# Counting equal entries instead of gathering 47 columns of values, and no power operation behind gathers once the table is whole

## The chip, the cores and the metric

The kernel runs on one core of a Trainium2 chip. Such a core has TensorE (PE; its weight loads are PEld), VectorE (DVE), ScalarE (ACT), GpSimd (POOL) and SyncE (SP), which only issues DMAs here. The metric is the device time of one execution in microseconds; lower is better. A profile is one such execution, recorded by the hardware.

## The reference, cut to what matters

Two layers of a graph network over N = 2708 nodes with D = 128 features. `adj` is a dense 2708 x 2708 array, but only about five entries of a row (on average) are not zero: each row is a 0/1 mask with ones on the diagonal, divided by its number of ones. So all entries of a row that are not zero are the same number, the one on the diagonal.

```
# layer 0: hyperbolic aggregation, dense product with adj
XW = mobius_matvec(W, X); gamma = 2 / max(1 - |XW|^2, 1e-5)
two_mean = (adj @ (gamma * XW)) / clamp(adj @ (gamma - 1))
x = layernorm(x + expmap0(relu(logmap0(scale(two_mean)))))
# layer 1: messages over the pairs with adj[i, j] != 0
s = x @ msg_w[:, :D].T ; d = x @ msg_w[:, D:].T
messages = gelu(s[:, None, :] + d[None, :, :] + msg_b)      # i, j, d
aggregated = einsum('ijd,ij->id', messages, adj)
h = gelu(concat([x, aggregated]) @ upd_w.T + upd_b) + x
x = layernorm(x + layernorm(h) * ln_w + ln_b)
```

## The kernel before, in words

**Tiling.** The nodes lie in NB = 22 blocks of 128. `adj_t` is adj transposed by blocks with the diagonal set to zero; the diagonal itself comes as `dg`, one column for each block.

**Layer 0** (`layer0`, L362) takes one block b a turn: SP loads `aT` (128 x 2816, 1408 KB, two buffers of the pool `stream`), ACT takes its Sign (`sgn`, L367), and PE multiplies 22 pieces of `aT` with `y` (L372). Three calls of `layer0_end` (after blocks 10, 20 and 22) turn the sums into the new x, and write the product that every message needs as a row for each node into `table_dram` (L596, seven writes).

**Finding the pairs.** From `sgn`, `keys` (L388) and `extract` (L425) list the pairs (i, j) with adj[i, j] not zero, packed into 99 columns ("tiles") of 128 pairs. `LISTS` gives each list its number n of tiles and how many of them are `late`: the first n - late tiles hold only columns j below SPLIT*P = 1280, the late ones only columns from 1280 on. By the list `LATE` 48 of the 99 tiles are late. For each tile `extract` leaves `J` (the column), `rid` (the row), `same` (the value of row i's diagonal) and `F` (the flat address of adj[i, j], L513).

**Two gathers for each tile**, both indirect DMAs issued by POOL through `gather` (L197): `V` fetches adj[i, j], 128 single words, and `dd` fetches 128 rows of 512 bytes of `table_dram`. V is not used in the sum: at the end L895 compares V with `same`, and a mismatch sets a flag under which a dense loop does layer 1 over again (L905). The message uses `same` as the weight. Behind two of every three gathers stands an operation on POOL that only spends time: `gap`, a power of a 128 x 1 column (L205).

**When gathers go out.** In `extract`, V of a block below AT_ONCE = 12 goes out at once; that of later blocks is held in `values` and goes out one a turn (L815), two a message (L776), or when no rows are left to fetch (L734). Rows of early tiles need only the first 1280 rows of the table and start in block 14 (`fetch(6)`, L814). `whole` becomes true once the whole table is written in the source; only then are late rows fetched (L827). RING = 14 buffers of four tiles hold fetched rows.

**Messages** (`messages`, L741) take four tiles a turn: PE selects the s rows (L751), DVE builds the weighted selection `rv` (L753) and adds the gathered rows (L756), ACT applies Gelu (L757), PE sums into the nodes (L766). There are 25 such groups: 11 of the early tiles of blocks 0 to 13, then 14 of the rest. `node`, `update`, `first` and `finish` (L616 to L682) then do a block's update and its two normalisations, and write `out`.

**Order.** Each engine runs its instructions in the order that the framework's scheduler fixes at build time; it starts from the source's order, but lets instructions that are ready earlier go ahead. `tc.issue_after(ins)` holds instructions of an engine behind `ins`.

Of the kernel before, what the change touches and what calls it, by code (L numbers as in the profile page):

```python
# [28 lines left out]
CHUNKS = [(0, 10), (10, 20), (20, 22)]  # L29
PARTS = (0, 1, 2, 2)  # L30
GROUPS = [(0, 8), (8, 6), (14, 4), (18, 2), (20, 2)]
AT_ONCE = 12
EARLY = 14
FETCH = 14

# [46 lines left out]
def hyperbolic_then_message_kernel(  # L82
# [17 lines left out]
    LISTS, NT, NC = lists()  # L100
    CMAX = max(v[3] + v[4] for v in LISTS)
    NL = len(LISTS)
    TMAX = max(TILES)

    const = ctx.enter_context(tc.tile_pool(name="const", bufs=1))
# [62 lines left out]
    R = big.tile([P, NT, P], BF16, name="R")  # L168
    J = const.tile([P, NT], U32, name="J")
    V = const.tile([P, NT], F32, name="V")  # L170
    rv_of = const.tile([P, NT, 2], F32, name="rv_of")
    rid, same = rv_of[:, :, 0], rv_of[:, :, 1]
    top = const.tile([P, NC], F32, name="top")
# [6 lines left out]
    nc.gpsimd.memset(deg, 0.0)  # L180
    oe = const.tile([P, NL, 2], F32, name="oe")
    signs = const.tile([P, NB], F32, name="signs")
    poss = const.tile([P, NL], F32, name="poss")
    cap = const.tile([P, NL], F32, name="cap")
    least = const.tile([P, NL], F32, name="least")
# [11 lines left out]
    def gather(o, src, at, kind):  # L197
        last = nc.gpsimd.indirect_dma_start(  # L198
            out=o, out_offset=None, in_=src, in_offset=bass.IndirectOffsetOnAxis(ap=at, axis=0)
        )  # L200
        gathers[0] += 1
        latest[:] = [last.ins]
        if gathers[0] % 3:
            with tc.issue_after(last.ins), tc.high_priority():
                nc.gpsimd.tensor_tensor(gap[kind], half, half, op=OP.pow)  # L205

# [154 lines left out]

    def layer0(b):  # L362

        aT = stream.tile([P, NB, P], F32, name="aT")
        nc.sync.dma_start(aT, adj_t[b])
        sgn = stream.tile([P, NB, P], BF16, name="sgn")
        nc.scalar.activation(sgn, aT, AF.Sign, accum_out=signs[:, b : b + 1])  # L367
        op = bank("mp", 3)
        for j in range(NB):
            if j in BREAKS:  # L370
                yield
            p = nc.tensor.matmul(  # L372
                op[:, : D + 2], lhsT=aT[:, j, :], rhs=y[:, j, :], start=(j == 0), stop=(j == NB - 1)
            )
        products.append(p)

        nc.vector.scalar_tensor_tensor(
            nom[:, b, :], y[:, b, :], dg[:, b : b + 1], op[:, : D + 2], op0=OP.mult, op1=OP.add
        )
        v, t = nom[:, b, :D], small.tile([P, D], F32, name="junk")  # L380
        nc.scalar.activation(t, v, AF.Square, accum_out=ss[:, b : b + 1])
        t = small.tile([P, D], F32, name="junk_p", bufs=1)
        nc.vector.scalar_tensor_tensor(
            t, v, 0.0, v, op0=OP.max, op1=OP.mult, accum_out=sp[:, b : b + 1]
        )
        yield sgn
# [38 lines left out]
    def extract(l):  # L425
# [68 lines left out]
        for k0 in range(0, n, step):  # L494
# [18 lines left out]
            nc.vector.scalar_tensor_tensor(  # L513
                F[:, k0:k1], J[:, t], float(b * P * N - 1), rid[:, t], op0=OP.add, op1=OP.add
            )
        values.extend((t, F[:, t - t0 : t - t0 + 1]) for t in range(t0, t0 + n))
        if b < AT_ONCE:
            value(n)
        known[0] = b
# [152 lines left out]
    def node(h, k, b, b0, n, more, pool=fin):  # L672
# [7 lines left out]
        if k == n - 1:  # L680
            yield
            yield from finish(h, b0, n, pool, last=(b == NB - 1))  # L682

    queue = []

    def step(n=NB):
# [54 lines left out]
    def messages():  # L741

        q, ts = done[0], work[done[0]]
        done[0] += 1
        w = len(ts)
        dd = rooms[q][:, :w, :]
        X = bank("kx" if q >= ahead and q % 2 else "X").rearrange("p (t d) -> p t d", d=D)[:, :w, :]
        rv = edge.tile([P, 4, P], F32, name="rv", bufs=2)
        for k, (b, t, *_) in enumerate(ts):
            for i in range(3):  # L750
                nc.tensor.matmul(X[:, k, :], lhsT=R[:, t, :], rhs=s3[:, b, i, :], start=(i == 0), stop=(i == 2))  # L751

            nc.vector.tensor_scalar(  # L753
                rv[:, k, :], iotaN, rid[:, t : t + 1], same[:, t : t + 1], op0=OP.is_equal, op1=OP.mult
            )
        nc.vector.tensor_tensor(dd, X, dd, op=OP.add)  # L756
        nc.scalar.activation(dd, dd, AF.Gelu)  # L757
        for k, (b, t, first, final, before) in enumerate(ts):
            mine = before or b >= EARLY
            if first:  # L760
                while len(sums) > 2:
                    step()
                sums[b] = bank("mp", 3)
                if mine:
                    own(b, sums[b])
            nc.tensor.matmul(  # L766
                sums[b][:, :P], lhsT=dd[:, k, :], rhs=rv[:, k, :], start=(first and not mine), stop=final
            )
            if final and before:
                nc.scalar.copy(gd[:, b, :D], sums.pop(b)[:, :P])  # L770
            elif final:
                g0, gn = group[b]
                queue.append(node(gd[:, g0 : g0 + gn, :D], b - g0, b, g0, gn, [gd[:, b, :D]] if b < EARLY else []))
        fetch()
        if not whole:
            value(2)  # L776
        step()
        step(1)

# [9 lines left out]
    with tc.issue_after(setup.ins):  # L789
        for b in range(NB):  # L790
            block = layer0(b)
            next(block)
            go_on(b, 0)
            for x in placed:
                next(x, None)
            placed = []
            next(block)
            go_on(b, 1)
            for x in found:
                next(x)  # L800
            placed, found = found, []
            sgn = next(block)
            for l in of_block[b]:
                keys(l, sgn)
                found.append(extract(l))
            if b == 0 or b == NB - 1:
                for x in found:
                    next(x)
                    next(x, None)
                for x in placed:  # L810
                    next(x, None)
                found, placed = [], []
            if b >= FETCH:
                fetch(6)  # L814
                value(1)  # L815
            for b0, b1 in CHUNKS:
                if b == b1 - 1 and b1 < NB:
                    ends.append((b1, layer0_end(b0, b1)))
                    next(ends[-1][1])
    for _, e in ends:  # L820
        for _ in e:
            pass
# [64 lines left out]
    while done[0] < len(work):  # L887
        messages()
    value(NT)
    while queue:  # L890
        step()


    differ = small.tile([P, 4 * P], F32, name="work", bufs=3)[:, :NT]
    nc.vector.tensor_tensor(differ, V, same, op=OP.not_equal)  # L895
    nc.vector.scalar_tensor_tensor(differ, rid, 0.0, differ, op0=OP.is_gt, op1=OP.mult)
    other = small.tile([P, 3], BF16, name="db")
    nc.vector.tensor_reduce(other[:, 0:1], differ, axis=AX.X, op=OP.max)
    bp = bank("sel", 1)
    nc.tensor.matmul(bp[:, 0:1], lhsT=ones_b, rhs=other[:, 0:1], start=True, stop=True)  # L900
    flag = sc.tile([P, 1], I32, name="flag")
# [3 lines left out]
    with tc.If(dense > 0):  # L905
        with tc.tile_pool(name="dn", bufs=1) as dn:
            room = R.rearrange("p t i -> p (t i)").bitcast(F32)
            dT, sT = (flat(stream.tile([P, NB, P], F32, name="aT")) for _ in range(2))
            agT, row = (room[:, k * NP : (k + 1) * NP] for k in range(2))
            ge = flat(mx)  # L910
            nc.vector.memset(agT, 0.0)
# [95 lines left out]
```

## Time and profile before

| what | us |
|---|---|
| median of 3 runs | 397.85 (396.5 to 399.37) |
| the profiled execution | 396.73 |
| its span, first to last instruction | 395.0 |
| POOL busy | 290.8 |
| PE busy | 286.8 |
| DVE busy | 280.8 |
| ACT busy | 215.7 |
| last matmul of layer 0 (L372) starts | 217.8 |
| last write of the table is issued | 257.96 |
| first Gelu of a message (L757), last one | 241.6, 361.6 |

How to read it: the span is cut by engines that wait for each other, so busy shares are averages over stages with different limits; the chain of waits that ended last, and the engines' order of time in each stage, say more. In the lines shown below, a group has the source line, the engine, the operation, the tile that is written and those that are read, the count, the busy time and the mean, and the idle time of the engine just before with what ended it. The TensorE clock is a share of full speed. Line numbers are those of the kernel before.

### The profile page before, as it was taken

What the parts mean: (1) busy time and instruction counts of PE and PEld (TensorE: products, weight loads), DVE (VectorE), ACT (ScalarE), POOL (GpSimd) and SP (SyncE); (2) the same over time, 40 slices, a digit from 0 to 9 for tenths busy, and PEclk for the clock granted to TensorE, in tenths of its full rate; (3) what the DMA queues carried; (4) which work ended last, traced back from release to release, by engine and by line L of the source; (5) the groups of instructions that cost most, each with busy time, mean ns of one, the idle gap of its engine ahead of it and who ended that gap; (6) DMA issues with size and microseconds to landing.
All of it is one profiled execution on the core that took longest, in us unless ns stands there. A gap on an engine that the chain in (4) does not pass through costs nothing.

```text
span 395.0 us, 8366 instructions
## 1 busy us (share of the span) xinstructions
PE 286.8 (73%) x2616; PEld 255.7 (65%) x2616; DVE 280.8 (71%) x1579; ACT 215.7 (55%) x614; POOL 290.8 (74%) x424
## 2 busy tenths in 40 slices
PE   3418989989998999899998287399738569738100
PEld 3307988888987879788888266298636459626000
DVE  0798889977668979667579989877534547559632
ACT  2982676878757859777767469254212222242201
POOL 5500188888888883788888888888888888888830
PEclk9856999999999999989999778689887997975555
DMA  8800554444454545455662122101111111130101
GB/s 308 338 1 2 182 205 170 177 153 147 170 216 180 191 156 183 161 187 168 220 251 65 41 55 75 33 15 36 41 42 40 40 42 41 42 95 15 40 0 52
DMA packets 16031, 45.17 MB, mean 114 GB/s; under 512 B 5418, under 2 KB 10942, under 8 KB 13166
## 3 DMA queue, kind: packets, MB, share of 16 engines
q1 hardware_dynamic: 9502, 37.43, 25.9%
q0 software_dynamic: 6336, 6.55, 7.0%
q10 hardware_dynamic: 144, 0.60, 0.5%
q8 instruction: 22, 0.36, 0.3%
q14 instruction: 27, 0.22, 0.2%
HBM read 41.74 MB, written 2.83 MB: 113 GB/s over the span
## 4 chain that ended last, share of the span: by engine, by line
POOL 31%; PE 23%; DVE 20%; DMA 10%; issue 8%; ACT 5%; another core or an unknown queue 1%; DVEq 0%; POOLq 0%; ACTq 0%
POOL dd L198 14%; POOL gap L205 9%; PE mp L372 9%; POOL V L198 8%; DMA dd<-table_dram,J 6%; PE mp L766 3%; PE sel L501 3%; PE kx L399 2%; DMA table_dram<-dt 2%; DVE top L407 2%; DVE dd L756 2%; DMA xT<-in_x_t_dram 1%; ACT dd L757 1%; DMA V<-in_adj_dram,F 1%; PE sel L621 1%
## 5 line engine op out<-in xcount | busy, mean ns | idle before, releaser
L198 POOL DMA_INDIRECT V<-in_adj_dram,F x99 | 99.4, 1004 | 59.2 <-DVE F L513 38.2
L372 PE MATMUL mp<-y,aT 128*128 128x130 f32 x968 | 131.1, 286 | 0.3 <-issue 0.3
L372 PEld LDWEIGHTS mp<-y,aT 128*128 128x128 f32 x968 | 118.7, 195 | 0.9 <-issue 0.6
L198 POOL DMA_INDIRECT dd<-table_dram,J x99 | 98.1, 990 | 22.4 <-issue 19.7
L205 POOL TENSOR_TENSOR gap<-gap 128x1 f32<-128x1 f32 x132 | 82.3, 623 | 3.2
L367 ACT ACTIVATE sgn<-aT 128x2816 bf16<-128x2816 f32 x22 | 56.0, 2548 | 1.5 <-issue 0.9
L766 PE MATMUL mp<-rv,dd 128*128 128x128 f32 x198 | 35.0, 329 | 27.2 <-ACT dd L757 25.9
L766 PEld LDWEIGHTS mp<-rv,dd 128*128 128x128 f32 x198 | 29.8, 229 | 30.5 <-ACT dd L757 28.6
L399 PE MATMUL kx<-kd,sgn 128*128 128x128 bf16 x484 | 33.2, 224 | 8.1 <-ACT sgn L367 8.1
L399 PEld LDWEIGHTS <-sgn 128*128 128x128 bf16 x484 | 28.3, 100 | 14.4 <-ACT sgn L367 8.5
L757 ACT ACTIVATE dd<-dd 128x512 f32<-128x512 f32 (+1 forms) x25 | 15.6, 623 | 33.7 <-DVE dd L756 31.7
L753 DVE TENSOR_SCALAR rv<-iotaN,rv_of 128x128 f32<-128x128 f32 x99 | 30.7, 353 | 3.5 <-PE mp L766 3.5
L407 DVE MAX8 top<-kx 128x8 f32<-128x128 f32 (+3 forms) x133 | 25.4, 228 | 10.4 <-remote 5.5
L468 ACT ACTIVATE away<-iota,mid 128x256 f16<-128x256 f32 (+3 forms) x54 | 28.5, 571 | 3.8 <-DVE mid L461 2.9
L756 DVE TENSOR_TENSOR dd<-X,dd 128x512 f32<-128x512 f32 (+1 forms) x18 | 12.2, 679 | 20.6 <-DMA dd<-table_dram,J 19.7
L501 PE MATMUL sel<-z,R 128*128 128x42 bf16 (+5 forms) x297 | 19.3, 192 | 10.1 <-DVE R L473 5.3
L501 PEld LDWEIGHTS <-R 128*128 128x128 bf16 x297 | 15.0, 96 | 14.6 <-DVE R L473 7.3
L751 PEld LDWEIGHTS <-R 128*128 128x128 bf16 x297 | 21.6, 106 | 1.9 <-issue 0.3
L411 ACT ACTIVATE junk_s<-kx 128x384 bf16<-128x384 f32 (+2 forms) x25 | 12.1, 486 | 13.2 <-DVE top L407 10.4
L751 PE MATMUL X<-s,R 128*128 128x128 bf16 x213 | 18.6, 232 | 0.0
L756 DVE TENSOR_TENSOR dd<-kx,dd 128x512 f32<-128x512 f32 x7 | 4.8, 691 | 17.5 <-DMA dd<-table_dram,J 17.5
L506 DVE TENSOR_TENSOR work<-sel,place 128x120 f32<-128x120 f32 (+11 forms) x29 | 11.1, 384 | 8.5 <-PE sel L501 8.4
(226 smaller groups left out, 596.2 us busy)
## 6 DMA issues: line engine op xcount, KB each, us to landing
aT<-in_adj_t_dram SPq DMA_DIRECT2D x22, 1408.0 KB
V<-in_adj_dram,F POOLq DMA_INDIRECT x99
dd<-table_dram,J POOLq DMA_INDIRECT x99
xT<-in_x_t_dram SPq DMA_DIRECT2D x2, 704.0 KB
x_sb<-in_x_nm_dram SPq DMA_DIRECT2D x2, 704.0 KB
table_dram<-dt SPq DMA_DIRECT2D x4, 256.0 KB
out_dram<-nom SPq DMA_DIRECT2D x4, 256.0 KB
pk<-in_pack_dram ACTq DMA_DIRECT2D x1, 587.5 KB
```

Of the source, the lines that this page charges most:

```text
L198: last = nc.gpsimd.indirect_dma_start(out=o, out_offset=None, in_=src, in_offset=bass.IndirectOffsetOnAxis(ap=at, axis=0))
L205: nc.gpsimd.tensor_tensor(gap[kind], half, half, op=OP.pow)
L367: nc.scalar.activation(sgn, aT, AF.Sign, accum_out=signs[:, b : b + 1])
L372: p = nc.tensor.matmul(op[:, : D + 2], lhsT=aT[:, j, :], rhs=y[:, j, :], start=(j == 0), stop=(j == NB - 1))
L399: nc.tensor.matmul(kp[:, i * P : (i + 1) * P], lhsT=sgn[:, j, :], rhs=kd[:, q, :], start=False, stop=(i == len(groups) - 1 and j == j1 - 1),)
L407: nc.vector.max(top[:, c : c + 8], seg[:, s, :])
L468: nc.scalar.activation(r0, iota[:, k0 * P : k1 * P], AF.Abs, scale=2.0, bias=mid[:, k : k + 1])
L501: nc.tensor.matmul(sp[:, k, :], lhsT=R[:, t0 + k0 + k, :], rhs=z[:, i, :], start=(i == 0), stop=(i == 2))
L751: nc.tensor.matmul(X[:, k, :], lhsT=R[:, t, :], rhs=s3[:, b, i, :], start=(i == 0), stop=(i == 2))
L753: nc.vector.tensor_scalar(rv[:, k, :], iotaN, rid[:, t : t + 1], same[:, t : t + 1], op0=OP.is_equal, op1=OP.mult)
L756: nc.vector.tensor_tensor(dd, X, dd, op=OP.add)
L766: nc.tensor.matmul(sums[b][:, :P], lhsT=dd[:, k, :], rhs=rv[:, k, :], start=(first and not mine), stop=final)
```

## The change

Layer 0 also counts how many entries of each row are not zero (`deg`, from the keys). If all listed late pairs of row i have the value of the diagonal, then the number of entries of adj[i, 1280:] that equal `dg` is the number of late pairs of that row, plus one where the diagonal itself lies there. The change makes this comparison of counts in place of the V gathers of the late tiles.

- `values` no longer takes late tiles; `AT_ONCE = 22` sends the early ones' V out in `extract` for every block.
- `load` reads two row blocks of adj[:, 1280:] (128 x 1428 each, in rows of 5712 bytes) into one `aT` buffer by two DMAs on SP. Two loads stand in the source behind layer 0's loop; each `compare` issues the next.
- `compare`, once in each message after `whole`: the even block on DVE (`is_equal` with a sum), the odd one on ACT (Sign of the difference, then its Square with a sum). Eleven in all.
- At the end eight small DVE operations form `own_b` and join it to the flag; the comparison of V is masked to early tiles.
- `gap` is issued only while `whole` is not yet set, so the gathers after it follow each other directly.

```
--- before.py
+++ after.py
@@ -29,7 +29,7 @@
 CHUNKS = [(0, 10), (10, 20), (20, 22)]
 PARTS = (0, 1, 2, 2)
 GROUPS = [(0, 8), (8, 6), (14, 4), (18, 2), (20, 2)]
-AT_ONCE = 12
+AT_ONCE = 22
 EARLY = 14
 FETCH = 14
 
@@ -100,6 +100,7 @@
     LISTS, NT, NC = lists()
     CMAX = max(v[3] + v[4] for v in LISTS)
     NL = len(LISTS)
+    WIDE = max(NP, 2 * (N - SPLIT * P))
     TMAX = max(TILES)
 
     const = ctx.enter_context(tc.tile_pool(name="const", bufs=1))
@@ -168,6 +169,7 @@
     R = big.tile([P, NT, P], BF16, name="R")
     J = const.tile([P, NT], U32, name="J")
     V = const.tile([P, NT], F32, name="V")
+    nc.gpsimd.memset(V, 0.0)
     rv_of = const.tile([P, NT, 2], F32, name="rv_of")
     rid, same = rv_of[:, :, 0], rv_of[:, :, 1]
     top = const.tile([P, NC], F32, name="top")
@@ -180,6 +182,10 @@
     nc.gpsimd.memset(deg, 0.0)
     oe = const.tile([P, NL, 2], F32, name="oe")
     signs = const.tile([P, NB], F32, name="signs")
+    alike = const.tile([P, NB], F32, name="alike")
+    nc.gpsimd.memset(alike, 0.0)
+    if rows[-1] < P and NB % 2 == 0:
+        nc.gpsimd.memset(alike[:, NB - 1 :], float(N - SPLIT * P))
     poss = const.tile([P, NL], F32, name="poss")
     cap = const.tile([P, NL], F32, name="cap")
     least = const.tile([P, NL], F32, name="least")
@@ -200,7 +206,7 @@
         )
         gathers[0] += 1
         latest[:] = [last.ins]
-        if gathers[0] % 3:
+        if gathers[0] % 3 and not whole:
             with tc.issue_after(last.ins), tc.high_priority():
                 nc.gpsimd.tensor_tensor(gap[kind], half, half, op=OP.pow)
 
@@ -361,7 +367,7 @@
 
     def layer0(b):
 
-        aT = stream.tile([P, NB, P], F32, name="aT")
+        aT = stream.tile([P, WIDE], F32, name="aT")[:, :NP].rearrange("p (j i) -> p j i", i=P)
         nc.sync.dma_start(aT, adj_t[b])
         sgn = stream.tile([P, NB, P], BF16, name="sgn")
         nc.scalar.activation(sgn, aT, AF.Sign, accum_out=signs[:, b : b + 1])
@@ -513,7 +519,8 @@
             nc.vector.scalar_tensor_tensor(
                 F[:, k0:k1], J[:, t], float(b * P * N - 1), rid[:, t], op0=OP.add, op1=OP.add
             )
-        values.extend((t, F[:, t - t0 : t - t0 + 1]) for t in range(t0, t0 + n))
+
+        values.extend((t, F[:, t - t0 : t - t0 + 1]) for t in range(t0, t0 + n - late))
         if b < AT_ONCE:
             value(n)
         known[0] = b
@@ -681,6 +688,41 @@
             yield
             yield from finish(h, b0, n, pool, last=(b == NB - 1))
 
+
+
+    W = N - SPLIT * P
+    nats, seen = [], [0]
+    dneg = const.tile([P, NB], F32, name="dneg")
+    nc.vector.tensor_scalar_mul(dneg, dg, -1.0)
+
+    def load():
+
+        b = 2 * len(nats)
+        if b < NB:
+            nat = stream.tile([P, WIDE], F32, name="aT")
+            for k in range(2):
+                r = rows[b + k]
+                nc.sync.dma_start(nat[:r, k * W : (k + 1) * W], adj[(b + k) * P : (b + k) * P + r, SPLIT * P :])
+            nats.append(nat)
+
+    def compare():
+        u = seen[0]
+        if u == len(nats):
+            return
+        seen[0] += 1
+        nat = nats[u]
+        t = flat(stream.tile([P, NB, P], BF16, name="sgn"))
+        b, r = 2 * u, rows[2 * u]
+        nc.vector.tensor_scalar(
+            t[:r, :W // 2].bitcast(U8), nat[:r, :W], dg[:r, b : b + 1], None, op0=OP.is_equal, op1=OP.add,
+            accum_out=alike[:r, b : b + 1],
+        )
+        b, r = 2 * u + 1, rows[2 * u + 1]
+        o = t[:r, 1024 : 1024 + W]
+        nc.scalar.activation(o, nat[:r, W : 2 * W], AF.Sign, bias=dneg[:r, b : b + 1])
+        nc.scalar.activation(o, o, AF.Square, accum_out=alike[:r, b : b + 1])
+        load()
+
     queue = []
 
     def step(n=NB):
@@ -774,6 +816,8 @@
         fetch()
         if not whole:
             value(2)
+        else:
+            compare()
         step()
         step(1)
 
@@ -817,6 +861,8 @@
                 if b == b1 - 1 and b1 < NB:
                     ends.append((b1, layer0_end(b0, b1)))
                     next(ends[-1][1])
+    for _ in range(2):
+        load()
     for _, e in ends:
         for _ in e:
             pass
@@ -887,15 +933,28 @@
     while done[0] < len(work):
         messages()
     value(NT)
+
+    own_b = sc.tile([P, NB], F32, name="own_b")
+    nc.vector.tensor_copy(own_b[:, 1:], deg[:, NL - NB + 1 :, 2])
+    nc.vector.tensor_reduce(own_b[:, 0:1], deg[:, : NL - NB + 1, 2], axis=AX.X, op=OP.add)
+    nc.vector.tensor_scalar_add(own_b[:, SPLIT:full], own_b[:, SPLIT:full], 1.0)
+    if full < NB:
+        nc.vector.tensor_scalar_add(own_b[: rows[-1], full:], own_b[: rows[-1], full:], 1.0)
+    pairs = alike.rearrange("p (u k) -> p u k", k=2)[:, :, 1]
+    nc.vector.tensor_scalar(pairs, pairs, -1.0, float(W), op0=OP.mult, op1=OP.add)
+    nc.vector.tensor_tensor(own_b, own_b, alike, op=OP.not_equal)
     while queue:
         step()
 
 
     differ = small.tile([P, 4 * P], F32, name="work", bufs=3)[:, :NT]
     nc.vector.tensor_tensor(differ, V, same, op=OP.not_equal)
+    nc.vector.scalar_tensor_tensor(differ, limit, float(SPLIT * P), differ, op0=OP.is_lt, op1=OP.mult)
     nc.vector.scalar_tensor_tensor(differ, rid, 0.0, differ, op0=OP.is_gt, op1=OP.mult)
     other = small.tile([P, 3], BF16, name="db")
     nc.vector.tensor_reduce(other[:, 0:1], differ, axis=AX.X, op=OP.max)
+    nc.vector.tensor_reduce(other[:, 1:2], own_b, axis=AX.X, op=OP.max)
+    nc.vector.tensor_tensor(other[:, 0:1], other[:, 0:1], other[:, 1:2], op=OP.max)
     bp = bank("sel", 1)
     nc.tensor.matmul(bp[:, 0:1], lhsT=ones_b, rhs=other[:, 0:1], start=True, stop=True)
     flag = sc.tile([P, 1], I32, name="flag")
@@ -905,7 +964,7 @@
     with tc.If(dense > 0):
         with tc.tile_pool(name="dn", bufs=1) as dn:
             room = R.rearrange("p t i -> p (t i)").bitcast(F32)
-            dT, sT = (flat(stream.tile([P, NB, P], F32, name="aT")) for _ in range(2))
+            dT, sT = (stream.tile([P, WIDE], F32, name="aT")[:, :NP] for _ in range(2))
             agT, row = (room[:, k * NP : (k + 1) * NP] for k in range(2))
             ge = flat(mx)
             nc.vector.memset(agT, 0.0)
```

## Prediction, on record before the result

> **What bounds the kernel now.** I read the page first: whose chain ends last, and the costliest groups.
>
> ```profile
> span 395.0 us, 8366 instructions
> ...
> PE 286.8 (73%) x2616; PEld 255.7 (65%) x2616; DVE 280.8 (71%) x1579; ACT 215.7 (55%) x614; POOL 290.8 (74%) x424
> ...
> POOL 31%; PE 23%; DVE 20%; DMA 10%; issue 8%; ACT 5%; another core or an unknown queue 1%; DVEq 0%; POOLq 0%; ACTq 0%
> ...
> L198 POOL DMA_INDIRECT V<-in_adj_dram,F x99 | 99.4, 1004 | 59.2 <-DVE F L513 38.2
> ...
> L198 POOL DMA_INDIRECT dd<-table_dram,J x99 | 98.1, 990 | 22.4 <-issue 19.7
> L205 POOL TENSOR_TENSOR gap<-gap 128x1 f32<-128x1 f32 x132 | 82.3, 623 | 3.2
> ```
>
> POOL does three things: 99 one-word gathers (V), 99 row gathers (dd), and a small power operation behind two of every three. Then the waits of the whole span: who waits for POOL's results?
>
> ```profile
> POOL V L198 <- DVE F L513: 38.2, 3, 32.3
> DVE dd L756 <- DMA dd<-table_dram,J: 37.1, 12, 4.8
> ...
> DVE work L895 <- DMA V<-in_adj_dram,F: 8.1, 1, 8.1
> ```
>
> DVE waits twelve times for row gathers, and 8.1 us at the end for the last V. POOL itself waited 32.3 us only before it had work. POOL's timeline shows where this happens (start, duration, instruction, idle before it):
>
> ```profile
> 161.10 1.00 POOL L198 DMA_INDIRECT dd<-table_dram,J  x1 [0.95 <-DMA table_dram<-dt]
> 162.40 0.95 POOL L198 DMA_INDIRECT V<-in_adj_dram,F  x1 [0.30 <-DVE R L471]
> 163.65 0.94 POOL L198 DMA_INDIRECT V<-in_adj_dram,F  x1 [0.30 <-issue]
> ...
> 254.14 0.99 POOL L198 DMA_INDIRECT dd<-table_dram,J  x1 [0.17 <-issue]
> 255.15 0.60 POOL L205 TENSOR_TENSOR gap<-gap 128x1 f32<-128x1 f32 x1
> 255.92 0.99 POOL L198 DMA_INDIRECT V<-in_adj_dram,F  x1 [0.18 <-issue]
> ...
> 267.08 0.95 POOL L198 DMA_INDIRECT dd<-table_dram,J  x1 [0.30 <-issue]
> ...
> 355.04 0.96 POOL L198 DMA_INDIRECT dd<-table_dram,J  x1 [0.30 <-issue]
> 356.02 0.66 POOL L205 TENSOR_TENSOR gap<-gap 128x1 f32<-128x1 f32 x1
> 356.87 1.00 POOL L198 DMA_INDIRECT V<-in_adj_dram,F  x1 [0.19 <-issue]
> ...
> 378.56 0.99 POOL L198 DMA_INDIRECT V<-in_adj_dram,F  x1 [0.17 <-issue]
> ```
>
> From 161 us to 379 us POOL never rests: 44 "early" rows with 13 V until 255, 7 V until 267, 55 "late" rows from 267.08 to 355.04 (54 steps of 1.63 us), 14 V. The whole chip's end then hangs on the last V; the timeline of all engines:
>
> ```profile
> 372.97 0.16 DVE L629 TENSOR_SCALAR ve<-mv 128x2 f32<-128x2 f32 x1
> ...
> 381.24 0.26 DVE L895 TENSOR_TENSOR work<-V,rv_of 128x99 f32<-128x99 f32 x1 [8.11 <-DMA V<-in_adj_dram,F]
> ```
>
> DVE stops at 373.1 with the last normalisations queued behind the comparison of L895, and the run ends 13.8 us after it goes on. Last, how much room the other engines have, in 207 to 225, 240 to 255 and the late rows' two stretches (columns: PE, PEld, DVE, ACT, POOL busy us, clock, DMA share, GB/s):
>
> ```profile
> 207.00:225.00 18.00, 10.72 (x106) 9.84 (x105) 16.44 (x118) 12.06 (x35) 15.46 (x20) 0.91 0.20 63
> 240.00:255.00 15.00, 7.19 (x47) 5.89 (x47) 14.59 (x88) 9.27 (x28) 12.86 (x16) 0.69 0.14 41
> 278.00:312.00 34.00, 22.58 (x172) 19.45 (x173) 15.17 (x55) 8.00 (x24) 29.16 (x35) 0.85 0.17 40
> 312.00:356.00 44.00, 28.76 (x209) 24.37 (x208) 24.89 (x131) 12.79 (x37) 37.61 (x46) 0.87 0.22 54
> ```
>
> DVE is full while the table is finished, half empty while the late rows come.
>
> **What the Trainium skill says.** "DMA: Bandwidth & Descriptors", section "Queues, rings and completion order": within one issuing row a DMA engine consumes descriptors in ring order, and between rows it alternates packet by packet. The trace agrees with the first: the table write issued at 152.93, 0.7 us behind a 1408 KB block of aT on the same queue, was waited for 7.38 us. Same page, "SWDGE vs HWDGE vs iDMA": gather descriptors are written by GpSimd software; the trace has 0.94 to 1.0 us of POOL for each, whether it moves 4 B or 512 B a row. "ScalarE: Activation LUTs" puts cheap functions in every table set; the trace agrees for Square (L381 runs at 216.71 behind the Gelu load with no load of its own), so I charge Sign and Square no table loads.
>
> **Part 1: the value gathers.** V covered all 99 tiles; LATE sums to 48, so 51 stay. (The change's summary says 47; the lists give 48.) Up to block 11 they ran ahead of the table, where POOL waited for F anyway (5.77 us before 153.66): nothing gained there. Between 161 and 255 I count 13 V now, and 13 after it too (early tiles of blocks 10 to 20), so early rows still end near 255. What goes is the 7 V before 267 and the 14 after 355. The 14 free the end: DVE's stall of 8.1 us disappears, next late are the last normalisations themselves. The 7 filled a wait: the late rows need the whole table, whose last write is issued at 257.96.
>
> **Part 2: the power operations.** The 55 late rows lose theirs. A step without one shows in the trace: 161.10, 162.40, 163.65 are three gathers on end, 1.30 and 1.25 us. I take 1.28. A longer run than three is not shown: the bound below is 1.25, above it 1.40 if gathers pile up behind the new loads. 54 x (1.63 - 1.28) = 19 us.
>
> **Part 3: the counting.** Eleven loads of two 128x1428 blocks, 1.46 MB each (16 MB), eleven comparisons.
> DVE: L830 takes 0.681 us for 512 elements, L669 0.281 for 128, so 1.04 ns an element and 0.15 fixed: 1.64 for 1428, with the accumulator read (0.08, as L383) 1.72; x11 = 19 us.
> ACT: L367 takes 2.548 us for 2816, L757 0.628 for 512: 0.833 ns an element, 1.39 for 1428; Sign and Square and the read (0.19) are 2.97; x11 = 33 us.
> Loads: the same size as aT, so some 7 us each, two in flight, 5.2 to 7 us per comparison (two buffers each of 7.4 + 3.0 us give 5.2; 2.9 MB at the 206 GB/s that 161 to 207 moved give 7.0). The buffers of aT come free as blocks 20 and 21 end, near 210 and 217.8.
> This work has its source place behind the early messages, but the order on an engine is not the source's: L836, which stands after nearly all messages, ran at 250.6. So I expect comparisons as fillers from about 220 on, through about 275. Until 258 DVE is full, partly with such fillers (the L830 to L875 sums). I charge the table chain 1 us, bounds 0 and 10. The last table write then sits behind a load on SP's queue: 7.4 us instead of an estimated 2.5 (a gather's landing).
> So the first late row starts at 257.96 + 1 + 7.4 + 0.8 (start of POOL, as at 160.31 to 161.10) = 267.2: the V that filled the wait go, the wait stays. Bounds: 261.3 (quiet queue, no delay) and 276.
> Closing counts own_b: some eight small DVE operations at 0.17 us, 1.4 us, partly between others: 1 us. Setup memsets: POOL idles until 47. Nothing.
>
> **Sum.** Last late row 267.2 + 54 x 1.28 = 336.3. From the last row to the end, without the stall: (373.1 - 355.0) + (395.0 - 381.2) = 31.9. PE needs 51.3 us for the twelve groups of four between 278 and 356, 4.3 each, against 5.1 us in which four rows now come: close enough to slip, 2 us. With the 1 us of own_b the span is 371.2, 23.8 less. The profiled execution took 396.73 for its 395.0; the runs' median is 397.85, 1.1 more. So 372.9 on its scale, 374.1 on the median's; I say 373.
>
> **Rivals.**
> *Another engine takes over (0.17).* Groups of four come every 5.1 us but need DVE add, Gelu and PE one after another, with updates of 22 blocks between; at 5.7 us the thirteen groups from 281 end 8 us later: 381. For it: PE is busy 51.3 of 78 us at clock 0.86 already. Against: every group now waits for its rows, none for PE.
> *Everything hides (0.15).* Table in a quiet queue, late rows at 261.3, 1.25 us steps: last at 328.8, end at 361; time 363.
> *The comparison paces the messages (0.08, slower).* If the comparisons keep their source place, one behind each of messages 3 to 13, and in-order DVE and ACT wait for a load each time, then from 259: 4.6 us for two with loaded data, nine at P, eleven further groups at 4.3, and 26 from the last add (360.87, less the stall) to the end: 336.8 + 9P. It decides from P = 6.5; at 7.0 the span is 400 and the time 401.5. For it: 5.2 to 7.0 is what loads offer. Against: readiness orders these queues, and the first two loads are early.
> That the counts disagree and the dense loop runs would take 2708 turns of over 2 us (L367's size), milliseconds; equal neighbours are the same quotient as the diagonal, so 0.01, put to slower.
>
> **Numbers.** The forecast holds 0.59, with its neighbourhood 363 to 383. The range 360 to 388 takes in the first two rivals and leaves the slow ones and steps of 1.40 us with a late table out. About 1% is what a measurement can tell: faster 0.88, same 0.04, slower 0.08.
>
> **What would show it.** Right: 51 V and about 64 power operations; late rows from about 267 in steps near 1.28; no wait of L895; DVE waits for dd still the main ones after 280. Wrong: comparisons on DVE with waits for their loads between messages, POOL waiting for a free dd buffer, a table write later than 262, or steps over 1.4.

## The result: slower by 6%, and the profile after

| | before | after | ratio |
|---|---|---|---|
| median, us | 398.58 | 423.58 (419.56 to 425.65) | 1.062 [1.053, 1.072] |
| profiled execution, us | 396.73 | 424.86 | |
| its span, us | 395.0 | 423.2 | |

The forecast was 373, with a range from 360 to 388. Its counts came true: 51 V (so 48 columns went, not the 47 of the title), 64 power operations, late rows 1.25 us apart while POOL has a free buffer. The time went elsewhere. The page of the kernel after, whose line numbers all further lines use unless another kernel is named (the busy digits are tenths in 40 slices of 10.6 us):

```profile
PE 284.3 (67%) x2616; PEld 255.0 (60%) x2616; DVE 298.1 (70%) x1611; ACT 246.0 (58%) x647; POOL 198.3 (47%) x311
...
PE   3419989998999999999944570930203528999720
...
DVE  0797989877689786765899999730012407989995
ACT  2981767867778698866787898830301413443532
POOL 6400485687430037888888870177770762000000
...
PE 49%; DVE 28%; another core or an unknown queue 14%; ACT 3%; issue 3%; DMA 1%; DVEq 0%; ACTq 0%
...
L204 POOL DMA_INDIRECT V<-in_adj_dram,F x51 | 51.1, 1002 | 93.2 <-DVE F L519 78.2
...
L795 DVE TENSOR_SCALAR rv<-iotaN,rv_of 128x128 f32<-128x128 f32 x99 | 30.6, 350 | 38.0 <-remote 31.8
...
L211 POOL TENSOR_TENSOR gap<-gap 128x1 f32<-128x1 f32 x64 | 40.4, 631 | 1.6
```

POOL lost 92 us of work and is no longer the bound. But look at slices 27 to 33 (275 to 349 us): beside POOL's 6s and 7s, PE, DVE and ACT show 0 to 5. The chain's entry for time without a known releaser ("remote" in the waits) has grown from 1% to 14%. The windows show it sharply (same columns as before the change; from 278 to 312 PE had 22.58 us of work before, and POOL 29.16):

```profile
278.00:312.00 34.00, 4.86 (x39) 3.71 (x37) 2.92 (x9) 4.38 (x6) 25.69 (x28) 0.59 0.21 53
...
279.00:298.00 19.00, 0.19 (x4) 0.01 (x1) 1.81 (x5) 0.00 (x0) 14.31 (x16) 0.64 0.21 53
...
317.00:324.00 7.00, 0.00 (x0) 0.00 (x0) 0.20 (x1) 0.00 (x0) 0.85 (x1) 0.50 0.07 19
324.00:334.00 10.00, 9.00 (x69) 8.37 (x68) 5.98 (x16) 4.62 (x12) 5.00 (x6) 0.76 0.12 29
334.00:347.00 13.00, 2.85 (x17) 2.24 (x16) 2.38 (x5) 2.28 (x7) 9.92 (x11) 0.56 0.21 56
351.00:404.00 53.00, 49.32 (x397) 42.64 (x396) 49.08 (x253) 23.34 (x71) 2.90 (x3) 0.92 0.05 15
```

From 279 to 298, 16 gathers went out and PE did four matmuls, with the DMA engines 21% busy. Most of the messages' work then happens from 351 to 404, with PE busy for 49 of 53 us: 118 of the 198 matmuls of L808. What did the engines wait for? The waits of the whole span (us in total, times, longest; POOL's waits for its first work stand ahead of these):

```profile
...
DVE rv L795 <- remote: 31.8, 3, 22.5
PEld L793 <- issue: 31.8, 9, 11.2
ACT nom L812 <- PE mp L808: 26.9, 7, 23.4
ACT nom L812 <- remote: 26.4, 3, 19.8
DVE dd L798 <- remote: 25.5, 3, 13.6
...
POOL dd L204 <- ACT nom L812: 16.9, 2, 9.6
POOL dd L204 <- DMA aT<-in_adj_dram: 14.9, 1, 14.9
```

Of the first five only `dd` (L798) needs gathered rows, and the DMA engines moved those in step (53 GB/s in the windows). `rv` (L795) and `nom` (L812) wait for matmuls alone. ACT's timeline and PE's, around one of the longest:

```profile
277.38 1.47 ACT L722 ACTIVATE sgn<-aT,dneg 128x1428 bf16<-128x1428 f32 x1
298.60 0.27 ACT L812 COPY nom<-mp 128x128 f32<-128x128 f32 x1 [19.75 <-remote]
```

```profile
277.55 1.14 PE L808 MATMUL mp<-rv,dd 128*128 128x128 f32 x8
...
298.92 0.58 PE L744 MATMUL mp<-ident,nom 128*128 128x128 f32 x1 [19.73 <-ACT nom L812]
```

The matmuls of L808 ended at 278.69 (the profile models where matmuls end); the copy that needs them began at 298.60. And PE, where it did have work, got an instruction about every 2 to 3 us, between gathers that kept their step (timeline of all engines):

```profile
303.49 0.27 PE L793 MATMUL kx<-s,R 128*128 128x128 bf16 x1 [1.96 <-issue]
304.43 0.94 POOL L204 DMA_INDIRECT dd<-table_dram,J  x1 [0.30 <-issue]
304.88 0.10 PEld L793 LDWEIGHTS <-R 128*128 128x128 bf16 x1 [3.38 <-issue]
305.59 0.26 PE L793 MATMUL kx<-s,R 128*128 128x128 bf16 x1 [1.84 <-issue]
```

So while gathers follow each other, the other engines go on many microseconds after what they need is done, as far as the profile shows it.

### The profile page after: what moved, and what is told of

Same layout as the page of the kernel before. It is cut to its first block, busy times and chain, and to the rows that moved or that the text cites. A ratio compares the mean times of both kernels' runs of the same rounds, so it can differ in the third digit from the quotient of the medians.

```text
span 423.2 us, 8342 instructions
## 1 busy us (share of the span) xinstructions
PE 284.3 (67%) x2616; PEld 255.0 (60%) x2616; DVE 298.1 (70%) x1611; ACT 246.0 (58%) x647; POOL 198.3 (47%) x311
## 4 chain that ended last, share of the span: by engine, by line
PE 49%; DVE 28%; another core or an unknown queue 14%; ACT 3%; issue 3%; DMA 1%; DVEq 0%; ACTq 0%
PE mp L378 19%; PE kx L405 7%; PE mp L808 6%; DVE sgn L716 3%; PE sel L507 3%; PE X L793 2%; PE sel L628 2%; DVE top L413 2%; PE sel L626 2%; PE X L597 2%; DVE rv L795 2%; PE kx L399 1%; DMA xT<-in_x_t_dram 1%; PE kx L793 1%
## 5 line engine op out<-in xcount | busy, mean ns | idle before, releaser
L204 POOL DMA_INDIRECT dd<-table_dram,J x99 | 95.7, 966 | 60.7 <-issue 25.1
L204 POOL DMA_INDIRECT V<-in_adj_dram,F x51 | 51.1, 1002 | 93.2 <-DVE F L519 78.2
L795 DVE TENSOR_SCALAR rv<-iotaN,rv_of 128x128 f32<-128x128 f32 x99 | 30.6, 350 | 38.0 <-remote 31.8
L793 PEld LDWEIGHTS <-R 128*128 128x128 bf16 x297 | 23.9, 117 | 33.4 <-issue 31.8
L211 POOL TENSOR_TENSOR gap<-gap 128x1 f32<-128x1 f32 x64 | 40.4, 631 | 1.6
L812 ACT COPY nom<-mp 128x128 f32<-128x128 f32 x14 | 3.7, 264 | 55.9 <-PE mp L808 26.9
L793 PE MATMUL X<-s,R 128*128 128x128 bf16 x213 | 21.7, 258 | 21.5 <-DVE dd L798 21.5
L808 PE MATMUL mp<-rv,dd 128*128 128x128 f32 x198 | 32.9, 320 | 3.8 <-ACT dd L799 3.8
L808 PEld LDWEIGHTS mp<-rv,dd 128*128 128x128 f32 x198 | 29.2, 227 | 5.1 <-ACT dd L799 4.3
L798 DVE TENSOR_TENSOR dd<-X,dd 128x512 f32<-128x512 f32 (+1 forms) x18 | 12.2, 683 | 27.3 <-remote 25.5
L744 PE MATMUL mp<-ident,nom 128*128 128x128 f32 x44 | 11.2, 362 | 28.3 <-ACT nom L812 19.7
L744 PEld LDWEIGHTS mp<-ident,nom 128*128 128x128 f32 x44 | 8.3, 246 | 29.5 <-ACT nom L812 19.9
L507 PEld LDWEIGHTS <-R 128*128 128x128 bf16 x297 | 15.2, 96 | 10.6 <-DVE R L479 5.8
```

The source lines that it names most:

```text
L204: last = nc.gpsimd.indirect_dma_start(out=o, out_offset=None, in_=src, in_offset=bass.IndirectOffsetOnAxis(ap=at, axis=0))
L507: nc.tensor.matmul(sp[:, k, :], lhsT=R[:, t0 + k0 + k, :], rhs=z[:, i, :], start=(i == 0), stop=(i == 2))
L744: nc.tensor.matmul(ag[:, :P], lhsT=gd[:, b, :D], rhs=ident, start=True, stop=False)
L795: nc.vector.tensor_scalar(rv[:, k, :], iotaN, rid[:, t : t + 1], same[:, t : t + 1], op0=OP.is_equal, op1=OP.mult)
L808: nc.tensor.matmul(sums[b][:, :P], lhsT=dd[:, k, :], rhs=rv[:, k, :], start=(first and not mine), stop=final)
```

## Experiments

Which of the two halves does it, and where? The runs came in six groups, each on another chip, and the groups are of two kinds, which turned out to be the main finding. In the first kind the kernel before takes 396 to 399 us (as in the result above), in the second 390 to 392. Ratios below are always to the kernel before on the same chip in the same group. No chip came up twice, so whether the chip or the occasion makes the kind is not shown; "kind of chip" below is short for both. The table is the summary, the texts follow.

| kernel | mean step of late rows, us | second kind | first kind |
|---|---|---|---|
| changed kernel | 1.26 unhindered | 0.931 | 1.062 |
| gap kept (counting alone) | 1.62 | 0.978, 0.980 | 0.980 |
| gap gone (no counting) | 1.26 | 0.939, 0.937 | not run |
| gap behind one of three | 1.43 | 0.956, 0.954 | 1.052 |
| memset of one column as gap | 1.27 | 0.928, 0.933 | 1.058 |
| memset of 540 columns as gap | 1.55 | 0.968 | 0.974 |

**The gap kept**, so the counting alone:

```
-        if gathers[0] % 3 and not whole:
+        if gathers[0] % 3:
```

> The changed kernel with the power operation kept behind two of three gathers to the end; the counting stays. Theory A (gathers that follow each other without a pause hold up the other engines): the long waits of DVE, ACT and PE between 279 and 350 us go; late rows start near 273 as now and come every 1.63 us, last at 361, and 32 us behind it the end: span about 394, ratio to before 0.98 to 1.00. Theory B (the 16 MB of loads and the comparisons hold up the messages): the power operation is idle time, the waits stay, ratio 1.05 or more.

Measured on a chip of the second kind: 383.19 against 391.39, 0.978 [0.973, 0.982]; late rows from 265.2 to 352.6. Counting is no loss.

**The gap gone alone**: the kernel before with the opposite edit.

```
-        if gathers[0] % 3:
+        if gathers[0] % 3 and not whole:
```

> The kernel before with one edit: no power operation once the table is whole; all 99 V gathers stay, no counting. Theory A: the same long waits appear as soon as late rows run on end, from about 270 us; ratio 1.02 to 1.08. Theory B: nothing is loaded or compared, so the gathers are only closer: late rows from 267, 68 steps of 1.25 us to the last V at 353, end 16 us later: span about 370, ratio 0.93.

Measured beside the last: 366.61, 0.939 [0.934, 0.944]. Late rows from 262.0 to 330.1, 55 on end, then 14 V, and PE keeps 13.6 to 14.6 of every 18 us busy meanwhile. This half, too, is a gain. Both halves gain and the whole had lost: a contradiction, unless something else differed.

**A gap behind one late row in three**, and **a memset of one column in place of the power operation** behind two of three:

```
-        if gathers[0] % 3 and not whole:
+        if gathers[0] % 3 if not whole else gathers[0] % 3 == 0:
```

```
-        if gathers[0] % 3 and not whole:
+        if gathers[0] % 3:
...
+                if whole:
+                    nc.gpsimd.memset(gap[kind], 0.5)
```

> The changed kernel with the power operation behind one of three gathers once the table is whole (runs of three gathers). Theory A, if three in a row are harmless: late rows from 273 every 1.43 us, last at 350, span about 383, ratio 0.96; if three in a row already hold up the others, the waits are back and the ratio is over 1.02. Theory B: as the changed kernel, 1.05 or more.

> The changed kernel with a memset of one column on POOL (0.09 us where the page shows it) in place of the power operation behind two of three gathers once the table is whole. Theory A1 (any other POOL instruction between gathers lets the others through): steps near 1.35 us, last row at 346, span about 379, ratio 0.95. Theory A2 (it is the time between gathers that counts): the pause is too short, long waits stay, ratio 1.03 to 1.07. Theory B: 1.05 or more.

Measured: 0.956 [0.952, 0.960] and 0.928 [0.924, 0.931], no standing engines in either. They seemed to say that any operation between gathers is enough. That was wrong, as the other kind of chip showed.

**The changed kernel again, and three cuts of it.** These ran on a chip where the kernel before took 398.12.

> The changed kernel itself, beside the next three. Theory C (the long waits belong to this program): ratio 1.04 to 1.08 and waits of 10 to 20 us between 279 and 350 again, in the same places. Theory D (they belonged to the occasion): ratio near 0.93, as with the short operation.

Measured: 423.85 (416.85 to 424.7). The stall is the same, with gathers on end from 274.9 to 318.6.

Without loads, comparisons and their counts (this kernel leaves out the check of the 48 tiles):

```
-        else:
-            compare()
...
-    for _ in range(2):
-        load()
```

> The changed kernel without loads and comparisons: late values are neither gathered nor counted, that part of the check is left out; no operation behind late rows. Theory E (back-to-back gathers need the loads or comparisons beside them to hold up the others): no long waits, late rows from 262 every 1.25 us, last at 329, end 32 us later: span 361, ratio 0.92. Theory F (they come whenever no other POOL instruction follows late rows, except where V gathers follow, as in the kernel before without its operation): long waits, ratio over 1.0.

Measured: 411.07, 1.029 [1.022, 1.036]. The engines stand without any counting (windows of this kernel):

```profile
280.00:298.00 18.00, 0.00 (x0) 0.00 (x0) 1.80 (x5) 0.00 (x0) 13.73 (x15) 0.53 0.23 55
```

With the loads but with comparisons of 8 columns (the counts are left out):

```
-            t[:r, :W // 2].bitcast(U8), nat[:r, :W], dg[:r, b : b + 1], None, op0=OP.is_equal, op1=OP.add,
+            t[:r, :4].bitcast(U8), nat[:r, :8], dg[:r, b : b + 1], None, op0=OP.is_equal, op1=OP.add,
...
-        nc.scalar.activation(o, nat[:r, W : 2 * W], AF.Sign, bias=dneg[:r, b : b + 1])
+        nc.scalar.activation(o, nat[:r, W : W + 8], AF.Sign, bias=dneg[:r, b : b + 1])
```

> The changed kernel with all loads, but each comparison on 8 columns (DVE and ACT 0.2 us each in place of 1.8 and 3.0); the counts are left out of the flag. If the loads bring the waits, they stay: ratio over 1.0. If the work on DVE and ACT does: gone, ratio 0.92 to 0.94.

Measured: 412.38, 1.036 [1.029, 1.042], with the same stall: neither loads nor comparisons cause it. First late row 261.1, against 274.9 with full comparisons on the same chip and 259.7 without counting: what delays the table is the comparisons, not the bytes of the loads.

The gap kept for the first 12 late rows only:

```
-        if gathers[0] % 3 and not whole:
+        late_n[0] += bool(whole)
+        if gathers[0] % 3 and late_n[0] <= 12:
```

> The changed kernel with the power operation kept behind two of three of the first 12 late rows only, while the last loads are still in flight; 43 rows then follow without one. Theory G (the waits start where back-to-back gathers meet loads in flight): none appear, late rows from 265, 12 at 1.6 and 43 at 1.25 us, last at 338, span about 370, ratio 0.945. Theory H (a long run of gathers is enough beside the counting's order of instructions): the waits come after the 12th, ratio over 1.0.

Measured: 423.27, 1.059 [1.052, 1.067]. The stall moved (windows of this kernel, 18 us each):

```profile
280.00:298.00 18.00, 7.97 (x81) 6.92 (x79) 7.20 (x19) 7.26 (x15) 15.12 (x19) 0.84 0.19 46
298.00:316.00 18.00, 8.05 (x51) 7.28 (x50) 4.77 (x13) 4.17 (x12) 13.73 (x15) 0.59 0.23 55
316.00:334.00 18.00, 0.00 (x0) 0.00 (x0) 0.00 (x0) 0.00 (x0) 13.43 (x16) 0.50 0.21 51
```

With the gap the engines run; when it ends the work thins out, and from 316 on nothing but POOL moves for 18 us. It is the gathers on end, then, wherever they stand. But then the gap-gone kernel should have stalled, unless the two groups differ in something else.

**Four kernels once more, together on one chip.**

> The changed kernel itself, so that it stands on one chip beside the three that follow. Theory of the program (gathers that follow each other with nothing between them hold up the other engines' completions, on any chip): 1.06 of before, with stretches of 10 us and more after the first late row in which TensorE, VectorE and ScalarE all stand. Theory of the chip (some chips do it, some do not): 1.06 where before takes 398, and about 0.92 (some 360 us) with no such stretch where before takes 391.

> Before, with no power operation behind the gathers of late rows and all values still gathered, again. Theory of the program: 0.94 of before and no standing engines, as the first time, so that what differs from the changed kernel is in the order of its instructions. Theory of the chip: where the changed kernel beside it stands still, this one does so too and comes out at 1.0 or above; where the changed kernel does not, 0.94.

> The changed kernel with a memset of one column in place of the power operation behind two of three late rows, again. Theory of the program: 0.93 of before, since an operation of any length between gathers is enough. Theory of the chip: 0.93 only where the changed kernel beside it has no standing engines; else above 1.0, since the short operation leaves the late rows at the same step of 1.25 us.

> The changed kernel with the power operation kept, so the counting alone, again. Both theories: 0.97 to 0.985 of before, with late rows 1.62 us apart and no stretch of standing engines; the theory of the chip would allow a second such result on a chip on which the changed kernel stands still, and this is what makes the gap, and not the counting, the cause there.

The chip was one of the second kind (390.31 before), and the changed kernel itself took 363.61, 0.931 [0.924, 0.939]. Gap gone 0.937 [0.928, 0.946], short memset 0.933 [0.926, 0.939], gap kept 0.980 [0.973, 0.986]. So it is the kind of chip, not a contradiction between the halves. The same program's page, digits as above (slices of 9 us) and the chain:

```profile
PE   2614999999999999999999807462794899994800
...
DVE  0699799987778897887678999999791898987994
ACT  1893467788866967999766896898792644335222
POOL 5700068568852200368888888883067777776000
...
PE 44%; DVE 23%; DMA 13%; issue 8%; ACT 7%; POOL 5%; DVEq 0%; SPq 0%; ACTq 0%; POOLq 0%
```

and its window for the same stretch as the first one after the change:

```profile
279.00:298.00 19.00, 16.60 (x138) 15.33 (x139) 16.92 (x55) 10.34 (x30) 14.43 (x16) 0.82 0.23 52
```

POOL does the same in both (16 instructions, 14.4 us, 52 GB/s), PE 138 matmuls instead of 4. No wait is put down to "remote" in this run.

**What in the gap matters, its presence or its time?** Two runs on a chip of the first kind (396.5 before).

> The changed kernel with a memset of one column in place of the power operation behind two of three late rows. On a chip on which before takes 391: 0.93, as twice already. On one on which before takes 398, two theories. Any instruction of GpSimd between two gathers is enough to let the other engines through: 0.92 to 0.94 and no stretch of standing engines. It is the time between the gathers that counts: at a step of 1.27 us the memset gives nearly none, so the engines stand as they do in the changed kernel, and it comes out at 1.0 to 1.06.

> The changed kernel with the power operation kept, so the counting alone. On a chip on which before takes 391: 0.98, as twice already. On one on which before takes 398: with the gap as the guard, 0.96 to 0.99 and no stretch of 10 us in which TensorE, VectorE and ScalarE stand; if the counting's own loads hold the engines up there, 1.0 or above, with late rows 1.6 us apart all the same.

The short memset: 419.18, 1.058 [1.050, 1.066], and the engines stand (its windows):

```profile
279.00:298.00 19.00, 0.00 (x0) 0.00 (x0) 0.69 (x1) 0.00 (x0) 15.22 (x26) 0.53 0.22 52
```

The gap kept, on the same chip: 388.91, 0.980 [0.974, 0.986], no such stretch, one "remote" wait, of 0.6 us. An operation between gathers is not enough; it was so on the second kind only because nothing is needed there.

**Time or kind, and how much.** A memset of 540 columns takes 0.58 us, nearly what the power operation takes (0.61):

```
+    pause = const.tile([P, 540], BF16, name="pause")
...
+                    nc.gpsimd.memset(pause, 0.5)
```

> The changed kernel with a memset of 540 columns behind two of three late rows, which should take about 0.6 us as the power operation does (99 columns took 0.17, one column 0.09 to 0.11). On a chip on which before takes 397, two theories. Time between the gathers is what frees the other engines: as with the power operation kept, 0.97 to 0.99, late rows 1.6 us apart on average, no stretch of 10 us in which the engines stand. The power operation does something of its own: the engines stand as in the changed kernel, 1.05 or more. On a chip on which before takes 391, 0.98 by both.

> The changed kernel with the power operation behind one of three late rows, a mean step of 1.44 us. On a chip on which before takes 397: if one pause of 0.6 us in 3.8 us is enough to let the other engines through, 0.96 and no standing engines, as on the other kind of chip; if each pair of gathers without a pause holds them up for its own length, something between 0.98 and 1.03, with waits of a few us in all three engines but none of 10.

This chip was of the second kind (391.75): 378.36, 0.968 [0.962, 0.973], and 373.37, 0.954 [0.950, 0.958]. Only the first kind can tell, so they ran once more:

> The same as i1, a memset of 540 columns behind two of three late rows, once more because the first landed on a chip on which before takes 392. Where before takes 397: 0.965 to 0.985 and no standing engines if it is time that frees the engines; 1.05 or more, standing engines, if the power operation did something of its own.

> The same as i2, the power operation behind one of three late rows. Where before takes 397: 0.96 and no standing engines if one pause of 0.6 us in 4.3 us is enough; 0.98 to 1.03 with waits of a few us if each stretch without a pause costs its own length; 1.05 if only a pause behind two of three is enough.

First kind (398.71). The long memset: 388.89, 0.974 [0.971, 0.978], with "remote" waits of 2.5 us at most. One gap in three: 419.89, 1.052 [1.048, 1.056], all three engines at half pace (its windows):

```profile
298.00:316.00 18.00, 9.71 (x51) 8.27 (x51) 4.54 (x11) 5.08 (x13) 14.60 (x17) 0.50 0.19 44
316.00:334.00 18.00, 7.60 (x29) 6.30 (x30) 4.61 (x17) 2.19 (x7) 14.75 (x17) 0.50 0.20 48
```

So it is time, not the kind of operation. A mean step of 1.55 us is enough on the first kind, 1.43 is not. (Whether the mean counts, or that no more than two gathers follow each other without a pause, these two don't separate.) The first kind stays behind even then, 388.89 against 378.36 for this kernel. Part of that comes before any late row: the last matmul of layer 0 starts at 206.2 to 209.5 us in the runs of the second kind and at 212.6 to 220.0 in those of the first.

**A reading of the size.** POOL stops by itself when it has no free buffer (`POOL dd L204 <- ACT nom L812` above), and the others don't come back at once. After the change the last gather of the first 36 starts at 316.90:

```profile
316.90 0.94 POOL L204 DMA_INDIRECT dd<-table_dram,J  x1 [0.30 <-issue]
323.80 1.29 DVE L798 TENSOR_TENSOR dd<-X,dd 128x512 f32<-128x512 f32 x2 [13.58 <-remote]
```

From the first gather of this burst (273.10) to 323.80 are 50.7 us for 36 rows, 1.41 us a row. Worked out in the same way, the changed kernel again gives (325.55 - 274.89) / 36 = 1.41, the one without counting (305.01 - 259.67) / 32 = 1.42, the short memset (312.91 - 268.61) / 32 = 1.38. This is how a backlog looks that is worked off at some 1.4 us a row while POOL adds to it every 1.25, and a step of 1.55 us lies clear above that. One of 1.43 lies a little above it too and still had the engines at half pace, so gathers alone don't give the size. It is inferred from times. What the backlog is made of, why it holds up signals between PE, DVE and ACT, and what differs between the chips, no view shows: the DMA engines are 21% busy, the step and bytes of the gathers are the same on both kinds. That stays open.

**A rival that no run tests: the recording.** The two kinds also differ in how complete their profiles are. The page of each of the ten runs of the second kind gives a time from issue to landing for `aT`, the page of none of the ten of the first kind does, the kernel before included. The changed kernel on the first kind, then on the second:

```profile
aT<-in_adj_t_dram SPq DMA_DIRECT2D x22, 1408.0 KB
aT<-in_adj_t_dram SPq DMA_DIRECT2D x22, 1408.0 KB, 6.4
```

A landing time is given only where all events of the landings are in the trace. Counted there, the 150 gathers of this kernel left 2334 such events on the second kind and 830 on the first; of the signals of DVE's 1309 instructions that send one, 1303 and 1132 are recorded. So single "remote" labels on the first kind are to be read with care. The empty windows stand without them, since the traces hold the same number of instructions (8342). Something that carries these events falls short on the first kind, before the gathers without a gap begin and with the gap too. Whether it is the recorder alone, and whether the recorder takes part in the stall, is not shown: each run on record has a span and a granted clock, and none is known to be timed without a recording.

## Why the prediction was wrong, step by step

**Bound, counts, the engines' prices of counting: right.** DVE's comparison (L716) took 1.70 us and its read 0.08, forecast 1.72 together; ACT's two passes 1.48 and 1.39 and the read 0.19, forecast 2.97. They ran early, as fillers, from 215; the last of them were then caught in the stall, to 334 on both engines. The wait of the last comparison of V is gone. Counting alone, with the gap kept, gained 2% on both kinds of chip.

**Counting's price for the table: mis-sized twice, and hidden.** The forecast charged the chain to the table 1 us (bounds 0 and 10), and 8.2 us from the last write to the first late row. The writes before, then after, with the first late row (first and last start stand behind the durations):

```profile
L596 SPq DMA_DIRECT2D table_dram<-dt x7: 360/376/389, 144.0 to 258.0; - x7
...
L603 SPq DMA_DIRECT2D table_dram<-dt x7: 360/377/801, 142.5 to 268.4; - x7
...
273.10 0.94 POOL L204 DMA_INDIRECT dd<-table_dram,J  x1 [14.91 <-DMA aT<-in_adj_dram]
```

The last write is 10.4 us later, and the first late row follows it after 4.7. A table write later than 262 was one of the forecast's own signs of being wrong. The comparisons cost it: with 8 columns the last write goes out at 258.4, with whole ones on the same chip at 269.4. The same delay is there on the second kind: from the last matmul of layer 0 to the last write are 51.8 us in the changed kernel and 40.1 in the gap-gone one beside it.

**Part 2 failed.** "A step without one shows in the trace" priced the removal at what the gap costs on POOL, 54 x (1.63 - 1.28) = 19 us of gain with nothing set against it, and its upper bound of 1.40 us asked only whether the gathers themselves would slow down. They did not: 1.25 us, the lower bound. What was not priced is what the gap keeps free for the others, on the first kind of chip. The trace before could not show that: the longest stretch of gathers without a gap that the prediction found was three. But 82.3 us of POOL on an operation whose result nobody reads was the row to be suspicious of.

The miss, by the terms of the sum (span 423.2 against 371.2, 52.0 us):

| term | forecast | first kind | second kind |
|---|---|---|---|
| first late row | 267.2 | 273.1 | 263.2 |
| 54 steps | 69.1 | 83.9 | 68.2 |
| last late row to the end | 34.9 | 66.2 | 29.6 |
| span | 371.2 | 423.2 | 361.0 |

On the first kind the first term is 5.9 late, within its bounds of 261.3 and 276 by the luck of two errors that partly cancel. The steps lost 14.8, in POOL's two waits for buffers (9.6 and 7.3 us) that the stalled messages held, not in the step; such waits, too, were on the forecast's list of signs. The tail lost 31.3: the message work that had not been done beside the gathers and came after them. 46 of the 52 us are thus the stall.

On the second kind the size comes out: ratio 0.931, forecast 373 / 397.85 = 0.938. No engine stands, the steps are the forecast's lower bound, and the tail is 5.3 us shorter. Part of that is luck. The forecast was made from a kernel whose layer 0 ended at 217.8; here its last matmul starts at 206.9, and this about pays for the delay of the table. Its numbers are also those of the rival "everything hides": last late row at 328.8 forecast and 331.4 measured, span 361 and 361.0. That is luck too: a later row and a shorter tail cancel, and the undelayed table of that rival did not happen.

**The rivals.** The slower one that was on record, comparisons pacing the messages through late loads, did not happen: DVE sat idle for 0.0 us before its comparisons, and on the same kind of chip the gap kept gains. The true slower case was missing from the list; on the first kind its price is 46 us, and its point of decision lies between 1.43 and 1.55 us a row.

**Parts don't add up exactly.** Beside each other on the second kind, counting alone gives 8.0 us, the gap alone 23.6, both 26.7. Likely, but only argued: without the power operation the 14 V behind the late rows are cheaper too (331.3 to 347.7 in the gap-gone kernel, 356.9 to 378.6 before), so there is less left for counting to save.

**What to run.** For an unknown chip the long memset with the counting is the best that was measured: 0.968 on the second kind and 0.974 on the first, the only one beside the gap kept (0.978 to 0.980) that gains on both. The two never ran on one chip, and on the first kind their intervals overlap. On the second kind alone the changed kernel or the short memset, 0.928 to 0.933.

## What to carry to other kernels

An instruction that computes nothing on the busiest engine may pace something that no view names; before removing it, ask what runs beside it, and let the range reach to the case that all of that stops. When two halves of a change gain and the whole loses, run the whole again beside the halves on one chip before looking for an interaction. A gain or loss from denser gathers holds only where it was measured; here that means with the two kinds of chip told apart, and with the question open of what a run without a recording takes.

## What the runs showed of the hardware

- The six groups of runs, each on its own chip, fell into two kinds: three with the kernel before at 396 to 399 us (first) and three at 390 to 392 (second). Gathers of 128 rows of 512 B at 1.25 us on end left TensorE, VectorE and ScalarE at work in the second (PE busy 16.6 of 19 us) and standing for some 20 us at a time in the first (PE busy 0.2 of 19). Chip, occasion and the part of the recording are not told apart.
- In the first, 0.58 to 0.61 us of other POOL work behind two of three gathers keeps the engines going; 0.12 us behind two of three, or 0.6 us behind one of three, does not.
- A stall of this kind shows as waits for "remote" or "issue" behind work that had ended (19.75 us for a matmul that was done at 278.69), with low DMA use (0.21), and as "another core or an unknown queue" in the chain. The profiles of that kind also lack part of the events (830 landing events of 150 gathers, against 2334).
